# A graph layer on one core: edge windows fetched ahead of x, and the first 24 gathered rows prepared one pass earlier

## The chip, the cores and the metric

The kernel runs on one core of a Trainium2 chip. A core has five engines with instruction streams of their own: TensorE (PE, matrix products), VectorE (DVE), ScalarE (ACT), GpSimd (POOL) and SyncE (SP), which here only issues DMA transfers. They share an on-chip memory (SBUF) and the accumulators that PE writes (PSUM); transfers to and from DRAM run on 16 DMA engines. Semaphores order all of it. The metric is the device time of one execution in microseconds (us); lower is better.

## The reference

```python
h = jnp.maximum(_layernorm(x, axis=-1), 0.0)          # x: 6250 x 128
x_i, x_j = h[dst], h[src]                             # 206250 edges, sorted by dst
msg = jnp.concatenate([x_i, x_j - x_i], -1) @ W.T + b # W: 128 x 256
out = jax.ops.segment_max(msg, dst, num_segments=6250)
return x + jnp.where(jnp.isfinite(out), out, 0.0)
```

The product splits: a message is A[dst] + B[src] with A = h (W1 - W2)^T + b and B = h W2^T. A is the same for every edge of a node, so the kernel needs, for each node, the largest B row over its source nodes, and adds A and x at the end. Every node has an edge to itself.

## The kernel before, in words

Each of the 128 partitions (lanes) owns 49 neighbouring destination nodes (LD) and with them one window of 1792 neighbouring edges (WIN). For each edge a DVE or PE route takes the maximum:

- **Staging of edges** (lines 176 to 285, 477 to 498). The starts of the windows are counted from loads of dst (line 181, count on ACT at 271). Two indirect transfers of POOL fetch the source and destination numbers of every window (284 `swin`, 285 `dwin`). Keys follow (483 to 498): source divided by Q = 50 (quotient l and remainder q), destination relative to the lane. ACT writes the quotient in f32 (`big`, 483) with its bias `kbias`, DVE rounds it (490) and goes on in 16 bits.
- **Comparisons** (528 to 580). Edges of a lane that have the same destination and the same quotient collide. 41 shifted comparisons on DVE (`shift`, 535) are summed by PE into `dup` (524); between them stand, by a list written out by hand (`among`), the layer norm's statistics (`moments`, 292; `scales`, 298), and small steps of the normalisation and product (`micro`, taken by `ln`).
- **Normalisation and product** (416 to 475). For each pair of the 50 columns q: ACT normalises (`scaled`), PE transposes (`turn`), PE multiplies (`product`), ACT copies out; `remainder` writes the second half of a split of B. B goes to `Bt` in DRAM (448 to 460), A to `XA` in DRAM. Both pass through the four halves of `stage`. The bias comes as one more matmul (433), from `bsel` and `brow`. x is added to XA by an accumulating transfer of POOL (`add_x`, 444), group by group of ten columns, once SP has written the group; the last group's stands at line 702.
- **Compaction** (592 to 725). ACT takes the sign of `dup` (594), a scan counts (609), and 11 passes (`pass_`, 624) move the edges that collided to the front of each lane: bit i of the distance is done in pass i. Up to 420 of them (GR) are handled by gathering. Before pass 6 (EP), `early` (637) takes the first 48 (EW) aside: it joins 14 blocks (SETS) in a tree (651 to 654), writes the index `ridx` (655) and issues 48 gathers.
- **Gathered edges.** `gather_group` (144) issues up to 8 indirect transfers (line 87), each one row of B per lane, into a ring of 48 places (6 groups, GB) in `X`; `stream_step` (151) takes the running maximum on DVE (157) and sends it to `M` in DRAM (164). A place is used again when its steps are done. x itself lies in the same memory `X` before.
- **The other edges** are taken by products with one-hot matrices in the main loop: 325 pairs, each with one-hot columns (905, 906), four matmuls (983) and one DVE maximum (989). `more_rows` (922) weaves stream steps and gathers in: 10 steps before the loop (971), then up to a limit that grows with the pair (990). From row 206 on, gathers of finished rows of M into `R` (919) join POOL's queue.
- **The end** (1002 to 1024). The last rows are gathered, XA is read, results are transposed, combined and stored.
- **Checks** of the input's shape write `badc` (380, 384, 397, 737 to 764); if any fails, a slow path (1030) runs. It doesn't run here. `tick` (506) is a small PE load.

Every engine works its own list in the order written. SP's begins with dst, x's first ten columns (193), W, b, then copies that wait for `swin` and `dwin` (340), then the other x columns (342).

Of the kernel before, what the change touches and what calls it, by code (L numbers as in the profile page):

```python
# [8 lines left out]
F32 = mybir.dt.float32  # L9
# [10 lines left out]
P = 128  # L20
# [33 lines left out]
def gnn_kernel(tc, x, src, dst, W, b, out):  # L54
# [17 lines left out]
    EP = 6  # L72
    EW = GB * U
    SETS = (WIN - EW - (1 << EP)) // (2 << EP) + 1
    assert EW + (1 << EP) <= 2 << EP and SETS <= 16 and WIN % (2 << EP) == 0
# [17 lines left out]
    with ExitStack() as ctx:  # L93
# [13 lines left out]
        with ExitStack() as body:  # L107
# [58 lines left out]
            with ExitStack() as pre:  # L166
# [16 lines left out]
                bsrc = pool.tile([33, C], F32, name="bsrc")  # L183
# [60 lines left out]
                kbias = pool.tile([P, 1], F32, name="kbias")  # L244
                bsel = pool.tile([P, L], F32R, name="bsel")
                brow = pool.tile([P, 2 * C], F32R, name="brow")
                V.memset(kbias, (1 - Q) * 0.5 / Q)
                V.memset(bsel.bitcast(F32), 0.0)
                V.memset(brow.bitcast(F32), 0.0)
                for r in (0, 32):  # L250
                    V.memset(bsel[r:r + 1].bitcast(F32), 1.0)
# [33 lines left out]
                gather(dwin, dst.rearrange("(e o) -> e o", o=1), begin_i[:, 0:1])  # L285

# [27 lines left out]
                for r in (0, 32):  # L314
                    V.tensor_copy(brow[r:r + 1, C:], bsrc[r:r + 1])
                V.tensor_tensor(brow[32:33, C:], bsrc[32:33], brow[32:33, C:].bitcast(F32), ALU.subtract)
# [5 lines left out]
                moments(0, GQ)  # L322
                scales(0, GQ)()
                V.tensor_copy(identb, ident)
                neg = pool.tile([P, P], BF16, name="neg")
                V.tensor_scalar_mul(neg, identb, -100.0)
                negb = pool.tile([P, P], BF16, name="negb")
                V.tensor_scalar_mul(negb, identb, -1.0)
# [3 lines left out]
                V.tensor_copy(IQ, row[:, 0, :Q].rearrange("p (q o) -> p q o", o=1).to_broadcast([P, Q, NBLK]))  # L332
                V.tensor_copy(IL, row[:, 1, :LD].rearrange("p (q o) -> p q o", o=1).to_broadcast([P, LD, NBLK]))
                for i in range(NBLK):
                    V.tensor_scalar_add(IW[:, :, i], row[:, 1, :WN], float(near[i]))
                V.tensor_scalar(nbias, row[:, 0], -2.0, -1.0, op0=ALU.mult, op1=ALU.add)


                for j, w_ in enumerate((swin, dwin)):
                    S_.dma_start(SC[j:j + 1], w_[:1, :1])  # L340
# [102 lines left out]
                def add_x(q0):  # L443
                    G_.dma_start(out=XA_l[:, q0:q0 + GQ], in_=x_l[:, q0:q0 + GQ], accum_op=ALU.add)  # L444

                def remainder(k):
# [8 lines left out]
                    if o + 2 == GQ or q0 + GQ == Q and o + 2 == GQ - 4:  # L455
                        for to, j in ((Bt_l, g), (XA_l, 2 + g)):
                            for p0, p1 in PARTS:
                                S_.dma_start(to[p0:p1, q0 + o0:q0 + o + 2], stage[p0:p1, j, o0:o + 2])
                        if q0 + GQ < Q:
                            add_x(q0)  # L460
# [12 lines left out]
                scaled(0)  # L473
                ln(2)

# [7 lines left out]
                A_.activation(big, sq, AF.Identity, scale=1.0 / Q, bias=kbias)  # L483
                A_.activation(s16, sq, AF.Identity, bias=nthr)
                V.tensor_scalar(d16, dwin, nthr, None, op0=ALU.add)
                V.tensor_scalar(dlc, d16, 0.0, float(LD + 1), op0=ALU.max, op1=ALU.min)
                dlc64 = eq[0].bitcast(I16)
                lq = eq[1].bitcast(I16)
                V.tensor_scalar(dlc64, dlc, 64.0, None, op0=ALU.mult)
                V.tensor_scalar(vm, big, MAGIC, -(MAGIC + L), op0=ALU.add, op1=ALU.add)  # L490
                V.tensor_scalar(lq, vm, float(-Q), None, op0=ALU.mult)
                V.tensor_tensor(q2, s16, lq, ALU.add)
                V.tensor_tensor(KA[:, 64:], dlc64, q2, ALU.add)
                ln(2)
                A_.activation(big, sq, AF.Copy, scale=float(1 << PB))
                ln(2)
# [68 lines left out]
                among[4] += [sel_rows]  # L565
                later = {}
                for q0, at_ in ((GQ, (1, 2, 3, 5)), (2 * GQ, (8, 10, 11, 13)), (3 * GQ, (17, 19, 20, 22)),
# [5 lines left out]
                for i in range(1, 41):  # L573
                    among[i].append(lambda: ln(1))
# [16 lines left out]
                less = junk[0]  # L591
                for i in range(2):
# [3 lines left out]
                make_sel(30, 40)  # L596

# [39 lines left out]
                def early():  # L637
# [3 lines left out]
                    F, FM = (swin[:, j * 16 * EW:(j + 1) * 16 * EW].rearrange("p (m w) -> p m w", w=EW) for j in range(2))  # L641
# [15 lines left out]
                    for _ in range(GB):  # L657
# [23 lines left out]
                for i in range(5):  # L681
                    rest[i].append(lambda i=i: ln(4 if i < 4 else len(micro)))
# [13 lines left out]
                for i in range(11):  # L696
# [3 lines left out]
                    for f in rest[i]:  # L700
                        f()
                add_x(Q - GQ)
# [15 lines left out]
                                op1=ALU.bitwise_and)  # L718
                sdl = u[:, OV:GR + OV]
# [5 lines left out]
                V.tensor_scalar(s, s, -0.5, FMAX, op0=ALU.add, op1=ALU.mult)  # L725
                make_sel(40, Q)
# [4 lines left out]
                spread_begin()  # L731
                finite(w_sb, 2 * C, P, 18)
                finite(bsrc[:1], C, 1, 20)
                found()
                apart()
# [3 lines left out]
                V.tensor_scalar(badc[:, 4:5], over_, 0.0, None, op0=ALU.is_lt)  # L739
                V.tensor_tensor(less[:, 1:], d16[:, 1:], d16[:, :WIN - 1], ALU.is_lt)  # L740
# [11 lines left out]
                for v, op, o in ((VMAX, ALU.is_lt, badc[:L, 16:17]), (-VMAX, ALU.is_gt, badc[:L, 17:18])):  # L752
                    V.tensor_scalar(fin_[:L, :Q], mv[:, :, 1], v, None, op0=op, op1=ALU.add, accum_out=o)
                    V.tensor_scalar(o, o, -1.0, float(Q), op0=ALU.mult, op1=ALU.add)
                tick(8)

                sdl_f = pool.tile([P, 1], F32, name="sdl_f")
                heads = pool.tile([P, 2], F32, name="heads")
                V.tensor_copy(sdl_f, sdl[:, :1])
# [340 lines left out]
```

## Time and profile before

| | us |
|---|---|
| median of three runs | 774.2 |
| lowest and highest | 771.93 and 775.31 |
| the profiled execution | 775.43 |
| its span, first to last instruction | 773.6 |
| mean granted clock of TensorE | 0.943 |

The profile comes from one execution. A row of a timeline gives start, duration, engine, line, operation, what is written and read, and in brackets the idle time of the engine just before and what is inferred to have ended it. A row of groups gives count, busy time and mean duration in ns, then the idle time before. L87 is the line of a helper, so all gathers stand under it and are told apart by names.

### The profile page before, as it was taken

What the parts mean: (1) busy time and instruction counts of PE and PEld (TensorE: products, weight loads), DVE (VectorE), ACT (ScalarE), POOL (GpSimd) and SP (SyncE); (2) the same over time, 40 slices, a digit from 0 to 9 for tenths busy, and PEclk for the clock granted to TensorE, in tenths of its full rate; (3) what the DMA queues carried; (4) which work ended last, traced back from release to release, by engine and by line L of the source; (5) the groups of instructions that cost most, each with busy time, mean ns of one, the idle gap of its engine ahead of it and who ended that gap; (6) DMA issues with size and microseconds to landing.
All of it is one profiled execution on the core that took longest, in us unless ns stands there. A gap on an engine that the chain in (4) does not pass through costs nothing.

```text
span 773.6 us, 11963 instructions
## 1 busy us (share of the span) xinstructions
PE 642.1 (83%) x3643; PEld 466.6 (60%) x3643; DVE 720.9 (93%) x1304; ACT 482.9 (62%) x1035; POOL 504.0 (65%) x522
## 2 busy tenths in 40 slices
PE   0799884649999898899989898999989898996860
PEld 0455553537667676666767666766767576775750
DVE  6999799987999999999999999999999999997773
ACT  3655683226789999565666657575666667674500
POOL 4000003877777777777777777777777777777764
PEclk9999997759999999999999999999999999998875
DMA  6542444123443433334343243434343233433593
GB/s 196 133 101 67 101 104 108 46 61 94 109 116 103 117 104 92 104 106 116 106 117 101 83 114 104 116 106 115 104 116 101 83 113 103 116 106 106 160 227 123
DMA packets 83699, 85.05 MB, mean 110 GB/s; under 512 B 9996, under 2 KB 71554, under 8 KB 83372
## 3 DMA queue, kind: packets, MB, share of 16 engines
q1 hardware_dynamic: 66951, 47.36, 21.7%
q0 software_dynamic: 16080, 35.93, 17.5%
q10 hardware_dynamic: 596, 0.92, 0.4%
q8 instruction: 30, 0.49, 0.3%
q14 instruction: 42, 0.34, 0.1%
HBM read 46.76 MB, written 40.47 MB: 113 GB/s over the span
## 4 chain that ended last, share of the span: by engine, by line
DVE 25%; PE 16%; issue 15%; ACT 9%; DMA 9%; POOL 3%; DVEq 0%; POOLq 0%
DVE acc L989 15%; PE ps L983 9%; DVE X L157 6%; DMA X<-Bt,ridx 6%; ACT oh L906 5%; PE z L905 4%; ACT counted L996 4%; DMA R<-M,last_e 3%; PE pv L837 2%; POOL X L87 2%; POOL R L87 1%; DVE OHQ L800 1%; DVE acc L987 1%; DVE OHD L807 1%; DVE OHD L804 0%
## 5 line engine op out<-in xcount | busy, mean ns | idle before, releaser
L87 POOL DMA_INDIRECT X<-Bt,ridx x420 | 440.7, 1049 | 131.7 <-issue 45.4
L906 ACT ACTIVATE oh<-z 126x490 fp32r<-126x490 f32 (+1 forms) x650 | 340.1, 586 | 162.6 <-PE z L905 161.3
L983 PE MATMUL ps<-oh,Bp 126*128 126x490 f32 (+1 forms) x1300 | 392.5, 425 | 40.1 <-DVE acc L989 38.9
L989 DVE TENSOR_TENSOR acc<-acc,ps 128x980 f32<-128x980 f32 (+1 forms) x312 | 361.1, 1157 | 8.3 <-PE ps L983 6.8
L983 PEld LDWEIGHTS ps<-oh,Bp 126*128 126x128 f32 x1300 | 239.3, 193 | 135.0 <-DVE acc L989 90.8
L905 PE MATMUL z<-Vb,Sel 128*126 128x490 f16 (+1 forms) x650 | 195.3, 375 | 12.4 <-ACT oh L906 9.7
L157 DVE SCALAR_TENSOR_TENSOR X<-X,slim 128x128 f32<-128x128 f32 x419 | 146.8, 350 | 9.2 <-issue 7.6
L905 PEld LDWEIGHTS <-Sel 128*126 128x126 f16 x650 | 86.8, 142 | 32.1 <-issue 3.9
L837 PEld LDWEIGHTS <-OHQ 128*128 128x128 bf16 x910 | 62.5, 161 | 17.8 <-issue 16.9
L837 PE MATMUL pv<-OHD,OHQ 128*128 128x28 bf16 (+1 forms) x896 | 67.2, 228 | 4.5 <-DVE OHD L807 4.4
L444 POOL DMA_DIRECT2D XA<-in_x x5 | 4.5, 902 | 94.3 <-DMA XA<-acc 94.3
L800 DVE TENSOR_TENSOR OHQ<-T,IQ 128x1092 bf16<-128x1092 bf16 (+5 forms) x104 | 62.2, 605 | 0.0
L87 POOL DMA_INDIRECT R<-M,last_e x49 | 48.3, 985 | 17.0 <-issue 11.3
L996 ACT ACTIVATE counted<-lane_dl,nbias 128x556 bf16<-128x556 int32 x50 | 42.6, 851 | 0.1
L524 PE MATMUL dup<-T,identb 128*128 128x512 bf16 (+1 forms) x168 | 39.8, 363 | 3.0 <-DVE T L535 2.8
L436 PE MATMUL pm<-wT,hT 128*125 128x256 f32 x100 | 27.7, 402 | 2.7 <-ACT hT L425 2.6
L524 PEld LDWEIGHTS <-identb 128*128 128x128 bf16 x168 | 16.2, 99 | 18.8 <-issue 6.4
L633 DVE COPY_PREDICATED pk<-big,pk 128x1927 int32<-128x1927 int32 (+12 forms) x13 | 22.9, 1759 | 0.4
L436 PEld LDWEIGHTS pm<-wT,hT 128*125 128x125 f32 x100 | 19.5, 198 | 6.1 <-ACT hT L425 3.7
L419 ACT ACTIVATE hs<-X,nmr,rstd 125x128 f32<-125x128 f32 x50 | 22.0, 494 | 0.5 <-DVE nmr L306 0.5
L535 DVE TENSOR_TENSOR T<-KA,KB 128x1792 bf16<-128x1792 int16 x21 | 21.5, 1081 | 0.2 <-PE dup L524 0.2
L535 DVE TENSOR_TENSOR T<-KA 128x1792 bf16<-128x1792 int16 x20 | 20.8, 1080 | 0.0
(272 smaller groups left out, 452.1 us busy)
## 6 DMA issues: line engine op xcount, KB each, us to landing
M<-X SPq DMA_DIRECT2D x52, 512.0 KB
X<-Bt,ridx POOLq DMA_INDIRECT x420, 2.5
XA<-in_x POOLq DMA_DIRECT2D x5, 625.0 KB, 6.1
ownb<-Bt SPq DMA_DIRECT2D x12, 245.0 KB
X<-in_x SPq DMA_DIRECT2D x5, 560.0 KB
Bt<-acc SPq DMA_DIRECT2D x4, 560.0 KB
XA<-acc SPq DMA_DIRECT2D x4, 560.0 KB
out_x<-R SPq DMA_DIRECT2D x8, 224.0 KB
```

The lines of the kernel that those rows point to most:

```text
L87: G_.indirect_dma_start(out=o, out_offset=None, in_=table, in_offset=bass.IndirectOffsetOnAxis(ap=idx, axis=0))
L157: V.scalar_tensor_tensor(G[:, j], state["prev"], slim[:, k:k + 1], G[:, j], op0=ALU.min, op1=ALU.max)
L436: T_.matmul(pm[:L, j], hT[k % 2][:, j, :L], wT, start=False, stop=j == 1)
L524: T_.matmul(dup[:, c0:c1], w, e[:, c0:c1], start=first, stop=last)
L535: V.tensor_tensor(e, KA[:, 64:], i1, ALU.is_equal)
L800: V.tensor_tensor(OHQ[:, :nl, a:z], over(TQ, z - a), iq, ALU.is_equal)
L837: T_.matmul(o, w, m, start=False, stop=True, skip_group_check=True)
L905: T_.matmul(z[:L + 1, :n], Sel[:, i + j], Vb[t % 2][:, :n], start=True, stop=True)
L906: A_.activation(oh[:, :n], z[:L + 1, :n], AF.Relu)
L983: T_.matmul(ps[:, j, :n], Bp[:, e, i + j], oh[j][:, :n], start=e == 0, stop=e == 1)
L989: V.tensor_tensor(a, a, ps[:, :, :n], ALU.max)
L996: A_.activation(counted.bitcast(BF16)[:, :NS], lane_dl, AF.Sign, scale=2.0, bias=nbias[:, c:c + 1], accum_out=ends[:, c:c + 1])
```

## The change

In the order of the program:

- SP loads W and b first; x's first ten columns come after the copy that waits for `swin`.
- The constants `identb`, `neg`, `negb`, `IQ`, `IL`, `IW` and `nbias` are made on DVE right after the edge windows are requested; the first statistics move from there into the comparisons (at 0 and 1), as do the first steps of the normalisation. Two steps are taken at every fifth comparison.
- The quotient is made by DVE from the integers into 16 bits; ACT's `big` for packing moves to comparison 7.
- The bias matmul, `bsel`, `brow` and `kbias` go. SP fills XA with 6250 copies of b, POOL adds x in five accumulating transfers, and each group of A is added from `stage` by one more accumulating transfer.
- `early` runs before pass 5 with 24 rows (EP 5, EW 24, SETS 28); the other 24 rows of the ring are requested after the final index.
- Some checks move: those on W and on the variances beside ACT's sign pass, the head count ahead of the last part of `Sel`.
- 4 stream steps run before the loop instead of 10; in the loop at least min(3k + 7, 16) are done after pair k.

```diff
-    EP = 6
-    EW = GB * U
+    EP = 5
+    EW = 3 * U
...
-                load_x(0)
                 S_.dma_start(w_sb, W)
-                for r in (0, 32):
-                    S_.dma_start(bsrc[r:r + 1], at(b, 0, [[C, 1], [1, C]]))
+                S_.dma_start(bsrc, at(b, 0, [[C, 1], [1, C]]))
...
                 gather(swin[:, :WIN], src.rearrange("(e o) -> e o", o=1), begin_i[:, 0:1])
                 gather(dwin, dst.rearrange("(e o) -> e o", o=1), begin_i[:, 0:1])
+                V.tensor_copy(identb, ident)
...
+                V.tensor_scalar(nbias, row[:, 0], -2.0, -1.0, op0=ALU.mult, op1=ALU.add)
...
-                moments(0, GQ)
-                scales(0, GQ)()
...
                 for j, w_ in enumerate((swin, dwin)):
                     S_.dma_start(SC[j:j + 1], w_[:1, :1])
+                    if j == 0:
+                        load_x(0)
                 for q0 in range(GQ, Q, GQ):
                     load_x(q0)
+
+                S_.dma_start(XA, at(b, 0, [[0, N], [1, C]]))
...
-                    T_.matmul(pm[:L], bsel, brow.rearrange("k (o c) -> k o c", o=1).to_broadcast([P, 2, 2 * C]),
-                              start=True, stop=False)
                     for j in range(2):
-                        T_.matmul(pm[:L, j], hT[k % 2][:, j, :L], wT, start=False, stop=j == 1)
+                        T_.matmul(pm[:L, j], hT[k % 2][:, j, :L], wT, start=j == 0, stop=j == 1, skip_group_check=True)
...
-                def add_x(q0):
+                for q0 in range(0, Q, GQ):
                     G_.dma_start(out=XA_l[:, q0:q0 + GQ], in_=x_l[:, q0:q0 + GQ], accum_op=ALU.add)
...
+                        if o + 2 == GQ:
+                            G_.dma_start(out=XA_l[:, q0:q0 + GQ], in_=stage[:, 2 + g], accum_op=ALU.add)
...
-                A_.activation(big, sq, AF.Identity, scale=1.0 / Q, bias=kbias)
+                V.tensor_scalar(l16, sq, 1.0 / Q, (1 - Q) * 0.5 / Q, op0=ALU.mult, op1=ALU.add)
+                V.tensor_scalar(lq, l16, float(-Q), float(Q * L), op0=ALU.mult, op1=ALU.add)
+                V.tensor_scalar(vm, l16, float(-L), None, op0=ALU.add)
...
+                among[7] += [lambda: A_.activation(big, sq, AF.Copy, scale=float(1 << PB))]
...
+                spread_begin()
...
+                finite(w_sb, 2 * C, P, 18)
...
-                    for _ in range(GB):
+                    for _ in range(EW // U):
                         gather_group()
...
-                add_x(Q - GQ)
...
+                for _ in range(GB - EW // U):
+                    gather_group()
...
-                more_rows(10)
+                more_rows(4)
...
-                    more_rows(GR * (k + 1 - wait) // (len(pairs) - wait - early))
+                    more_rows(max(GR * (k + 1 - wait) // (len(pairs) - wait - early), min(3 * k + 7, 16)))
```

More of the change, by code (lines that the diff above doesn't have):

```diff
@@ L725, in gnn_kernel @@
                 V.tensor_scalar(s, s, -0.5, FMAX, op0=ALU.add, op1=ALU.mult)
+                sdl_f = pool.tile([P, 1], F32, name="sdl_f")
+                heads = pool.tile([P, 2], F32, name="heads")
+                V.tensor_copy(sdl_f, sdl[:, :1])
+                V.tensor_scalar(mask[:, NS:NS + GR], sdl, sdl_f, None, op0=ALU.is_equal, op1=ALU.add, accum_out=heads[:, :1])
+                V.scalar_tensor_tensor(heads[:, 1:], heads[:, :1], float(P), lane, op0=ALU.mult, op1=ALU.add)
+                p = ps_m.tile([P, 512], F32, name="pm")
+                T_.matmul(p[:P - 1, :1], ident[:, 1:], heads[:, 1:], start=True, stop=True)
+                V.tensor_scalar(badc[:, 5:6], heads[:, :1], float(MENDK), None, op0=ALU.is_gt)
+                V.memset(mend_i, 0)
                 make_sel(40, Q)
```

90 lines of the change are left out of this document (29 added, 61 removed).

## The prediction

> **What bounds the kernel now.** The page says that VectorE (DVE) is busy most; what GpSimd (POOL) does between its instructions decides.
>
> ```profile
> span 773.6 us, 11963 instructions
> PE 642.1 (83%) x3643; PEld 466.6 (60%) x3643; DVE 720.9 (93%) x1304; ACT 482.9 (62%) x1035; POOL 504.0 (65%) x522
> ```
>
> POOL looks free at 65%. Its groups in the stretch from 200 to 700 us (count, busy us and mean ns, idle before) say otherwise:
>
> ```profile
> L87 POOL DMA_INDIRECT X<-Bt,ridx x357 | 370.6, 1038 | 108.8 <-issue 35.0 <-DMA X<-Bt,ridx 26.2 <-DVE acc L989 25.9
> L87 POOL DMA_INDIRECT R<-M,last_e x15 | 14.9, 993 | 4.6 <-issue 3.0 <-DMA X<-Bt,ridx 1.5
> L87 POOL DMA_INDIRECT mend<-M,mend_i x1 | 0.9, 940 | 0.3 <-DMA X<-Bt,ridx 0.3
> ```
>
> Busy and idle add up to 500.1 of the 500 us, and 108.8 / 357 is 0.30 us of idle per gather: 373 gathers stand back to back, each with 0.30 us of issue. Whatever the releaser column names, POOL waits for nobody. The windows (us, then busy of PE, PEld, DVE, ACT, POOL) put DVE beside it:
>
> ```profile
> 175.00:200.00 25.00, 25.00 (x149) 19.02 (x147) 19.98 (x26) 15.59 (x30) 19.41 (x20) 0.95 0.30 84
> 350.00:400.00 50.00, 45.42 (x262) 33.20 (x261) 49.90 (x85) 31.65 (x61) 38.72 (x38) 1.00 0.41 113
> ```
>
> DVE is full too. Which of the two ends last? The timeline of DVE late in the loop:
>
> ```profile
> 710.02 0.35 DVE L157 SCALAR_TENSOR_TENSOR X<-X,slim 128x128 f32<-128x128 f32 x1 [4.02 <-issue]
> 722.89 0.40 DVE L157 SCALAR_TENSOR_TENSOR X<-X,slim 128x128 f32<-128x128 f32 x1 [3.55 <-issue]
> ```
>
> DVE stands 4.02 and 3.55 us before a stream step, waiting for its row. So the chain that ends the run is POOL's: 420 gathers of X in one row from the first, then the gathers of R, the output. The end moves by what POOL's queue gains; what DVE gains beyond that becomes more such waits.
>
> POOL's queue begins here (POOL's timeline, and DVE's up to the index that releases it):
>
> ```profile
> 128.79 0.99 POOL L87 DMA_INDIRECT X<-Bt,ridx  x1 [4.07 <-ACT KB L678]
> 130.08 1.72 POOL L87 DMA_INDIRECT X<-Bt,ridx  x1 [0.31 <-issue]
> 134.79 2.97 POOL L87 DMA_INDIRECT X<-Bt,ridx  x1 [0.30 <-issue]
> 140.82 0.98 POOL L87 DMA_INDIRECT X<-Bt,ridx  x1 [0.30 <-issue]
> ```
>
> ```profile
> 119.80 1.15 DVE L632 TENSOR_SCALAR big<-pk 128x1896 int32<-128x1896 int32 x1
> 120.98 2.26 DVE L633 COPY_PREDICATED pk<-big,pk 128x1896 int32<-128x1896 int32 x1
> ...
> 127.58 0.21 DVE L653 COPY_PREDICATED swin<-swin 128x48 int32<-128x48 int32 x1
> 127.83 0.19 DVE L655 TENSOR_SCALAR ridx<-swin 128x48 int32<-128x48 int32 x1
> ...
> 129.86 1.12 DVE L632 TENSOR_SCALAR big<-pk 128x1864 int32<-128x1864 int32 x1
> ```
>
> The first gather follows `ridx` (128.02) by 0.8 us. ACT, named as releaser, is not among its inputs.
>
> **The change, part by part.**
>
> *Start.* DVE and SP now:
>
> ```profile
> 13.97 0.29 DVE L309 TENSOR_TENSOR w<-w_sb 128x128 f32<-128x128 f32 x1 [3.28 <-DMA w_sb<-in_L_gnn_W]
> 15.39 2.03 DVE L294 BATCH_NORM_STATS2 stats<-X 125x6 f32<-125x128 f32 x10
> 17.34 0.75 DVE L296 BATCH_NORM_AGGREGATE mv<-stats 125x2 f32<-125x6 f32 x10
> 18.47 0.22 DVE L305 RECIPROCAL rstd<-rstd 125x10 f32<-125x10 f32 x1 [0.37 <-ACT rstd L300]
> 18.80 0.22 DVE L324 CAST identb<-ident 128x128 bf16<-128x128 f32 x1
> 21.63 1.15 DVE L485 TENSOR_SCALAR d<-pk,nthr 128x1792 int16<-128x1792 int32 x1
> 22.82 0.63 DVE L486 TENSOR_SCALAR dlc__175<-d 128x1792 bf16<-128x1792 int16 x1
> 25.26 1.09 DVE L490 TENSOR_SCALAR vm<-big 128x1792 bf16<-128x1792 f32 x1 [1.15 <-ACT big L483]
> 29.91 2.09 DVE L535 TENSOR_TENSOR T<-KA 128x1792 bf16<-128x1792 int16 x2
> ```
>
> ```profile
> 16.80 0.25 SPq L340 DMA_DIRECT2D SC<-swin  x1
> 19.97 0.21 SPq L340 DMA_DIRECT2D SC<-pk  x1
> ```
>
> The SP copies wait for the two edge windows, so `swin` is there at 16.8 and `dwin` at 20.0. The constants (18.80 to 21.63, 2.83 us) go into the 3.28 us of idle ahead of 13.97 and are hidden. The keys now take 29.91 - 21.63 = 8.28 us; without the wait of 1.15 and the f32 `vm` of 1.09, with an int32 pass of 1.15 and an int16 one of 0.63, they take 7.8. They can start when `swin` lands. Two opposite effects bear on that: 0.64 MB of x no longer goes first, and the constants now run on DVE while POOL writes the descriptors of both gathers. I leave it at 16.8 (bounds 15.5 and 18.3). `dwin` is wanted 3.7 us after `swin`, later than 20.0. The first comparison then starts at 24.6, 5.3 earlier. The statistics of the first ten x columns (2.03 + 0.75 + 0.22 + about 0.2) move behind it, so 3.1 comes back: **2.2 us gained**, bounds 0.7 and 3.5. x itself now stands on SP behind the copy that waits for `swin`, and behind it wait the copy of `dwin`, the other x chunks, XA's fill and the Bt stores; it is issued at 17 and wanted near 26, and if it came later, DVE would stand. The dropped bias rows counted before 15.39; DVE now waits for `swin` at that place, so they bring nothing.
>
> *Comparisons.* DVE waits for TensorE (PE) twice, then for ACT's sign pass:
>
> ```profile
> 85.00 3.10 DVE L535 TENSOR_TENSOR T<-KA,KB 128x1792 bf16<-128x1792 int16 x3 [0.23 <-PE dup L524]
> 88.72 1.09 DVE L542 TENSOR_TENSOR T<-dlc__175 128x1792 bf16<-128x1792 bf16 x1 [0.62 <-PE dup L524]
> 93.52 0.35 DVE L598 TENSOR_SCALAR flow<-level,listed 128x128 f32<-128x128 f32 x1 [2.32 <-ACT T L594]
> ```
>
> PE loses one bias matmul per product, so the 0.85 us goes and PE's lag behind DVE shrinks a little: **1.0 us** (bounds 0 and 1.4). The checks moved into the 2.32 us wait take no time there and free about 1.7 us behind the passes, for DVE alone.
>
> *Early rows.* `ridx` for 24 rows is written without pass 5 in front (1.15 + 2.26 = 3.4 us) but with one level more in the tree (28 sets instead of 14: two instructions like the 0.21, 0.4 us). So POOL starts 2.2 + 1.0 + 3.4 - 0.4 = 6.2 us earlier. Beside passes 6 to 8 the second to fifth gathers took 130.08 to 140.82, 2.7 us each instead of 1.25. Pass 5 now lies beside gathers too: in its 3.4 us 1.3 get through instead of 2.7, **1.8 us lost** (bounds 0 and 3.4). The second half of the ring is issued after line 717's index, well before POOL has done 24. Bt's last store, already ahead of the first gather, moves with the normalisation chain and no longer shares its queue with XA's.
>
> *XA.* One accumulation stood among the gathers:
>
> ```profile
> 198.88 1.02 POOL L444 DMA_DIRECT2D XA<-in_x  x1
> 200.20 1.04 POOL L87 DMA_INDIRECT X<-Bt,ridx  x1 [0.30 <-DVE X L157]
> ```
>
> It goes: **1.0 us**. The ten accumulations of the new kernel are issued ahead of the first gather, in POOL's idle time; what waits behind them on POOL is the gathers, and the fill of XA that they wait for is a rival below.
>
> *Behind the passes (DVE only).* The head count's wait on PE goes, and fewer rows are run before the loop:
>
> ```profile
> 160.03 0.16 DVE L766 CAST mend_i<-pm 127x1 int32<-127x1 f32 x1 [1.18 <-PE pm L763]
> 171.99 3.44 DVE L157 SCALAR_TENSOR_TENSOR X<-X,slim 128x128 f32<-128x128 f32 x9
> ```
>
> DVE reaches the loop 2.2 + 1.0 + 1.7 + 1.2 - 0.4 = 5.7 us earlier, and six rows of 0.35 us move into the stretch where PE is full and DVE has 5 us idle (175 to 200): 7.8 in all. That is more than POOL gains, so POOL still ends last.
>
> **Sum:** 2.2 + 1.0 + 3.4 - 0.4 - 1.8 + 1.0 = 5.4 us. The profiled execution took 775.4 (its span 773.6 and 1.8 outside it) and would take 770.0; against the median of 774.2, **768.8**.
>
> **The rivals.**
>
> *The shared port costs more.* A gather beside pass 7 took 2.97 us, against 0.98 alone. If such passes stop POOL wholly, pass 5 costs 3.4 instead of 1.8, and the 2.83 us of constants delay both edge gathers by as much: 5.4 - 1.6 - 2.8 = 1.0 gained, 773.2. Against it: four gathers did finish beside three passes, and the constants are mostly small. The Trainium skill (SBUF — State Buffer, Who interferes with whom) states that a DVE instruction in a two-port mode or with two SBUF inputs and a GpSimd one hold the port exclusively, the second fully blocked. By that rule the sum is this rival's; the stretched gathers agree with a lock per instruction, not with a block through the whole stretch.
>
> *XA's chain holds the normalisation (slower).* XA is first filled with 6250 rows of bias; the five additions of x wait for that, and the first addition of a stage buffer for x's. ACT writes that buffer again for the eleventh pair of columns. Queue rows (packets, MB, share) of 20 to 32 us, which holds the last four of x's five loads, of 213 to 217 us (stores of 512 B rows) and of 52 to 59 us (one addition), and ACT's copy of that pair:
>
> ```profile
> q1 hardware_dynamic: 636, 2.55, 84.5%
> ```
>
> ```profile
> q1 hardware_dynamic: 1544, 0.78, 72.6%
> ```
>
> ```profile
> q0 software_dynamic: 144, 0.64, 53.7%
> ```
>
> ```profile
> 74.25 0.37 ACT L451 COPY acc<-pm 125x256 f32<-125x256 f32 x1 [0.59 <-PE pm L449]
> ```
>
> Packets of 512 B go at 1544 / (4 x 0.726) = 532 per us, so the fill takes 11.7 us behind x's load (near 31) and ends at 43; each addition takes 0.537 x 7 = 3.8 us, six with 2 us of latency 25: landed at 68, before 74. ACT waits from 74, PE two products (6 us) later, DVE three comparisons after that, at 83. So it decides once the fill ends after 58, at 2.3 times my rate; at three times it ends at 66, the addition lands at 91, and DVE loses 8: 777. The copies between two places in DRAM are not in this trace, hence its chance. The Trainium skill (DMA: Bandwidth & Descriptors, Why a DMA increments its semaphore by 16 and not by 1) lets a DMA use the largest number of engines up to 16 that divides its outer size, 10 for 6250; an estimate by it is 18.7 us, ending at 50, short of the point.
>
> *More.* Pass 5 costs gathers nothing and `swin` lands at 15.5: 5.4 + 1.8 + 1.3 = 8.5, 765.7.
>
> *It does not do what it says.* The keys start no earlier because the edges land as much later as they are wanted sooner; 5.4 - 2.2 = 3.2, 771.0.
>
> **How the numbers follow.** Forecast 0.55, port 0.15, XA's chain 0.13, more 0.10, no earlier keys 0.07. The measurement tells about 0.5%, 3.9 us, from no change. The forecast's terms leave it on the faster side four times in five (0.44); with "more" and a little of the others 0.56 faster. Slower is XA's chain and a remainder, 0.15; within 0.5%, 0.29. The range goes from 764.5, below "more", to 776, which leaves out most of XA's chain.
>
> **What would show it.** First comparison near 24.6; first gather of X near 122.6; the gathers from there to the last in one unbroken row, its last one near 718; DVE's waits before stream steps late in the loop longer than 4.02 and 3.55. ACT standing before L451 near 74 and DVE before L535 near 83 would show XA's chain. A first gather at 122 with an end that has not moved would prove wrong that POOL's queue sets the end.

## The result, and the profile after

The changed kernel takes 839.6 us (median of 4 runs, 838.13 to 840.56) against 773.9 (4 runs, 771.93 to 775.31): the ratio is 1.0849, with a 95% interval of 1.0819 to 1.0879. It is 66 us slower. The forecast was 768.8, its range 764.5 to 776.0, and the rival nearest to what happened gave 777.

The page of the profiled execution (839.02 us) begins so. The rows of slices cover 837.2 / 40 = 20.9 us with each figure.

```profile
span 837.2 us, 11852 instructions
PE 639.8 (76%) x3618; PEld 463.6 (55%) x3618; DVE 721.1 (86%) x1299; ACT 481.6 (58%) x1034; POOL 511.5 (61%) x527
...
DVE  7996011899988999999999999999999999999683
ACT  3463002683146799995757576666666666667320
POOL 4000020017777777777777777777777777777764
...
GB/s 181 148 37 37 36 144 150 61 100 50 65 88 80 108 101 91 120 100 95 98 116 104 126 103 110 102 110 101 110 98 114 98 114 98 110 102 122 120 236 132
```

DVE is as busy as before in microseconds (721.1 against 720.9), so it got no more work; standing was added. From the third to the fifth slice, about 42 to 105 us, the transfers move 37 GB/s, and from the fifth to the seventh, 84 to 147 us, DVE and ACT all but stand still. From there on the run looks as before: POOL's groups from 250 to 750 us in the changed kernel again fill the stretch, 0.30 us of idle per gather.

```profile
L87 POOL DMA_INDIRECT X<-Bt,ridx x358 | 369.8, 1033 | 109.1 <-issue 37.5 <-DMA X<-Bt,ridx 23.5 <-DVE acc L973 23.5
L87 POOL DMA_INDIRECT R<-M,last_e x15 | 16.5, 1098 | 4.6 <-DMA X<-Bt,ridx 2.4 <-issue 2.1
```

What stood? SP's timeline of the changed kernel (start, duration of the issue, line, transfer), where L331 is the fill of XA, L362 a small store of zeros and L444 the stores of B:

```profile
24.59 0.85 SPq L331 DMA_DIRECT2D XA<-in_L_gnn_b  x1
25.55 79.90 SPq L362 DMA_DIRECT2D Bt<-zero  x1
105.54 80.25 SPq L444 DMA_DIRECT2D Bt<-acc  x12
```

The fill itself is issued in 0.85 us. The next issue, a store of 11 KB, takes 79.90 us: SP gets it out at 105.45, when most of the fill is done. All stores of B are written behind it. POOL's, ACT's and DVE's timelines show who waits for the fill and for those stores (L431 adds x, L446 adds A, L428 and L438 copy into the four halves of `stage`, L305 is a step of the statistics, L516 a comparison, L523 the last one):

```profile
116.92 4.48 POOL L431 DMA_DIRECT2D XA<-in_x  x5 [100.92 <-DMA XA<-in_L_gnn_b]
...
190.81 0.99 POOL L87 DMA_INDIRECT X<-Bt,ridx  x1 [2.37 <-DVE ridx L643]
```

```profile
118.32 0.37 ACT L428 COPY acc<-pm 125x256 f32<-125x256 f32 x1 [45.93 <-DMA Bt<-acc]
139.37 0.37 ACT L438 COPY acc<-pm 125x256 f32<-125x256 f32 x1 [20.20 <-DMA XA<-acc]
```

```profile
16.13 1.09 DVE L470 TENSOR_SCALAR T<-swin 128x1792 int16<-128x1792 int32 x1 [2.31 <-DMA swin<-in_src,begin_i]
...
23.66 1.08 DVE L516 TENSOR_TENSOR T<-KA 128x1792 bf16<-128x1792 int16 x1
...
118.93 0.22 DVE L305 RECIPROCAL rstd<-rstd 125x10 f32<-125x10 f32 x1 [43.47 <-ACT rstd L300]
142.83 1.09 DVE L516 TENSOR_TENSOR T<-KA,KB 128x1792 bf16<-128x1792 int16 x1 [18.77 <-PE dup L505]
...
153.00 1.09 DVE L523 TENSOR_TENSOR T<-dlc__172 128x1792 bf16<-128x1792 bf16 x1 [0.39 <-PE dup L505]
```

The fill ends near 117 instead of 43. ACT stands twice: 45.93 us for a store of B, which is behind the fill on SP's queue, then 20.20 us for the addition to XA, which is behind the fill on POOL's. DVE stands 43.47 us for ACT, then 18.77 us for PE, which waits for ACT's copies. The last comparison starts at 153.00 instead of 88.72, 64.3 later, the first gather at 190.81 instead of 128.79, 62.0 later, and the last one at 786.84 instead of 722.97, 63.9 later. The whole loss lies before the gathers; behind them nothing is given back.

The rate of the fill: DMA queues of the changed kernel from 40 to 100 us (packets, MB, share of the 16 engines).

```profile
q1 hardware_dynamic: 4243, 2.17, 33.8%
```

4243 packets in 60 us are 71 rows of 512 B per us, where the forecast had 532 from stores out of SBUF. And the packets fill only a third of the time of 16 engines.

For some runs below the kernel before itself took 1064 to 1089 us on the same chip; their times are marked as not compared, and of their traces only what lies before the loop is used.

### The profile page after: what moved, and what is told of

Its sections match the earlier page's. It is cut to its first block, busy times and chain, and to the rows that moved or that the text cites. A ratio compares the mean times of both kernels' runs of the same rounds, so it can differ in the third digit from the quotient of the medians.

```text
span 837.2 us, 11852 instructions
## 1 busy us (share of the span) xinstructions
PE 639.8 (76%) x3618; PEld 463.6 (55%) x3618; DVE 721.1 (86%) x1299; ACT 481.6 (58%) x1034; POOL 511.5 (61%) x527
## 5 line engine op out<-in xcount | busy, mean ns | idle before, releaser
L967 PE MATMUL ps<-oh,Bp 126*128 126x490 f32 (+1 forms) x1300 | 393.0, 425 | 40.5 <-DVE acc L973 39.5
L889 PE MATMUL z<-Vb,Sel 128*126 128x490 f16 (+1 forms) x650 | 196.0, 376 | 12.9 <-ACT oh L890 10.3
L157 DVE SCALAR_TENSOR_TENSOR X<-X,slim 128x128 f32<-128x128 f32 x419 | 145.0, 346 | 7.6 <-issue 5.5
L431 POOL DMA_DIRECT2D XA<-in_x x5 | 4.5, 1579 | 100.9 <-DMA XA<-in_L_gnn_b 100.9
L505 PE MATMUL dup<-T,identb 128*128 128x512 bf16 (+1 forms) x168 | 42.8, 385 | 14.8 <-DVE T L516 14.8
L436 PE MATMUL pm<-Bp,negI 125*125 125x256 f32 x25 | 10.4, 414 | 48.6 <-ACT acc L428 48.6
L516 DVE TENSOR_TENSOR T<-KA,KB 128x1792 bf16<-128x1792 int16 x21 | 22.0, 1083 | 23.6 <-PE dup L505 23.6
L446 POOL DMA_DIRECT2D XA<-acc x5 | 4.8, 967 | 60.8 <-ACT Bp L439 56.3
L305 DVE RECIPROCAL rstd<-rstd 125x10 f32<-125x10 f32 x5 | 1.1, 210 | 43.6 <-ACT rstd L300 43.5
L428 ACT COPY acc<-pm 125x256 f32<-125x256 f32 x25 | 9.6, 383 | 45.9 <-DMA Bt<-acc 45.9
L436 PEld LDWEIGHTS pm<-Bp,negI 125*125 125x125 f32 x25 | 5.2, 208 | 52.4 <-ACT acc L428 51.4
L505 PEld LDWEIGHTS <-identb 128*128 128x128 bf16 x168 | 16.8, 105 | 31.5 <-issue 19.3
```

The costliest lines, as they stand in the source:

```text
L157: V.scalar_tensor_tensor(G[:, j], state["prev"], slim[:, k:k + 1], G[:, j], op0=ALU.min, op1=ALU.max)
L436: T_.matmul(pm[:L, :, :C], negI[:L, :L], Bp[:L, 0, 2 * k:2 * k + 2], start=False, stop=True, skip_group_check=True)
L505: T_.matmul(dup[:, c0:c1], w, e[:, c0:c1], start=first, stop=last)
L516: V.tensor_tensor(e, KA[:, 64:], i1, ALU.is_equal)
L889: T_.matmul(z[:L + 1, :n], Sel[:, i + j], Vb[t % 2][:, :n], start=True, stop=True)
L967: T_.matmul(ps[:, j, :n], Bp[:, e, i + j], oh[j][:, :n], start=e == 0, stop=e == 1)
```

## The experiments

**Which part costs the time.** Two kernels split the change: the kernel before with the XA part alone (`before_xa`), and the change without it (`xa_as_before`, run twice).

```diff
 # before_xa, on the kernel before
+                S_.dma_start(XA, at(b, 0, [[0, N], [1, C]]))
...
-                    T_.matmul(pm[:L], bsel, brow..., start=True, stop=False)
...
-                        for to, j in ((Bt_l, g), (XA_l, 2 + g)):
+                        if o + 2 == GQ:
+                            G_.dma_start(out=XA_l[:, q0:q0 + GQ], in_=stage[:, 2 + g], accum_op=ALU.add)
```

> The kernel before with only the change's XA part: no bias matmuls, XA filled from the one row of b in DRAM behind x's loads, ten POOL additions. Theory 1: it loses what the changed kernel lost, the fill ends near 118, ACT waits for Bt near 72, and the time is 835 to 850. If the loss needs another part of the change as well, it stays under 820.

> The changed kernel with its whole XA part undone: bias by matmul again, XA written by SP and x added by POOL group by group, as in the kernel before; all other parts of the change stay. Theory 1 (the fill of XA alone costs, through the queue behind it): no wait of DVE over 2 us among the comparisons, first gather of X near 122, 767 to 771 us. Theory 2 (another part of the change has a share of the 65 us): above 776 us.

> The changed kernel with its XA part undone, again, for its time. With the fill gone and one POOL addition back among the gathers (1.0 us) and the bias matmuls back (1.0 us), theory 1 gives 2 us more than the variant filled from SBUF: 768 to 773. If XA's ten additions cost something of their own in the other variant, this one is the faster of the two.

`before_xa` took 842.85 us in its one run, beside 773.96 (median of 23 runs) for the kernel before on the same chip: 68.9 more. Its two long ACT waits are those of the changed kernel (us in total, times, longest):

```profile
ACT acc L440 <- DMA Bt<-acc: 47.7, 1, 47.7
ACT acc L450 <- DMA XA<-acc: 21.1, 1, 21.1
```

`xa_as_before` took 1075.12 us against 1067.22 (not compared). `xa_as_before2` took 775.37 us (12 runs, 770.9 to 777.66), ratio 1.001, interval 0.9995 to 1.0025. So the XA part makes the whole loss, and the rest of the change brings nothing by itself, where my terms gave 5.4 - 1.0 (XA) - 0.85 (bias) = 3.5 us. Why nothing, this kernel's timelines show (POOL's first gathers, then two comparisons of DVE):

```profile
121.58 1.18 POOL L87 DMA_INDIRECT mend<-M,mend_i  x1 [3.89 <-DVE mend_i L642]
128.34 1.30 POOL L87 DMA_INDIRECT X<-Bt,ridx  x1 [5.58 <-DMA Bt<-acc]
```

```profile
24.87 1.08 DVE L528 TENSOR_TENSOR T<-KA 128x1792 bf16<-128x1792 int16 x1
...
89.12 1.09 DVE L535 TENSOR_TENSOR T<-dlc__173 128x1792 bf16<-128x1792 bf16 x1 [0.62 <-PE dup L517]
...
126.29 0.18 DVE L655 TENSOR_SCALAR ridx<-swin 128x24 int32<-128x24 int32 x1
```

The first comparison is 5.0 us earlier than before, the last one 0.4 later. The statistics that moved in between take 3.1 us of that, and with the bias matmuls still there and the steps of the product packed closer, DVE also waits 1.9 us for PE (0.85 before) and 1.1 us for ACT. And where the index is ready at 126.47, the gather waits until 128.34 for the last store of B. A new wait has taken the place of pass 5.

**The source of the fill.** The same 6250 rows of 512 B, but out of a copy of b in 125 partitions of SBUF, on the same queue at the same place (`fill_sbuf`, run twice).

```diff
+                S_.dma_start(bb, at(b, 0, [[0, L], [1, C]]))
...
-                S_.dma_start(XA, at(b, 0, [[0, N], [1, C]]))
+                for p0, p1 in PARTS:
+                    S_.dma_start(XA_l[p0:p1], bb[p0:p1].rearrange("l (o c) -> l o c", o=1).to_broadcast([p1 - p0, Q, C]))
...
-                S_.dma_start(bb, at(b, 0, [[0, L], [1, C]]))
```

> The changed kernel, but XA is filled with the same 6250 rows of 512 B from a copy of b in 125 partitions of SBUF, in two transfers, instead of from the one row in DRAM. Theory 1, with the source row in DRAM as what is slow: the fill ends near 45 us (532 rows per us as the stores of M), no wait of ACT for a Bt store, 766 to 771 us. Rival 1a (6250 rows are too many for one queue, whatever their source): the fill still takes over 60 us and the time stays above 815. Rival 1b (the ten accumulating transfers hold the stage buffers): the fill is short, but ACT waits over 5 us before its copies to stage, above 776.

> The changed kernel with XA filled from a copy of b in 125 partitions of SBUF, as before, on another chip for its time. The fill ended near 45 us in the first look, so ACT shouldn't wait for a Bt store nor DVE among the comparisons. If the fill was all that the change lost and my steps of the forecast hold, 766 to 771 us, with the first gather of X near 122. If the rest of the change brings nothing, within 3 us of the kernel before; if it loses too, above 777.

`fill_sbuf` took 1057.83 us against 1067.22 (not compared); POOL's additions start at 45.87. `fill_sbuf2` took 772.49 us (12 runs, 770.37 to 775.15), ratio 0.9978, interval 0.9966 to 0.9989. DMA queue from 34 to 40 us, and POOL, in its trace:

```profile
q1 hardware_dynamic: 3994, 2.04, 112.5%
```

```profile
45.39 4.48 POOL L433 DMA_DIRECT2D XA<-in_x  x5 [28.70 <-DMA XA<-bb]
```

3994 / 6 = 666 rows per us, a little over the forecast's 532. Beside the source only the load of that copy differs, which moves from late in the kernel to its start, and the 67 us are gone. So the fill's source is the cause, and the version with it is the only one here that beats the kernel before, by 0.2%.

**Engines or queue.** `fill_16` keeps the row in DRAM, and splits the fill so that 16 engines share it; `fill_act` only issues it from ACT's queue.

```diff
 # fill_16
-                S_.dma_start(XA, at(b, 0, [[0, N], [1, C]]))
+                K = N // 16
+                S_.dma_start(XA[:16 * K].rearrange("(a k) c -> a k c", k=K), at(b, 0, [[0, 16], [0, K], [1, C]]))
+                S_.dma_start(XA[16 * K:], at(b, 0, [[0, N - 16 * K], [1, C]]))
 # fill_act
-                S_.dma_start(XA, at(b, 0, [[0, N], [1, C]]))
+                A_.dma_start(XA, at(b, 0, [[0, N], [1, C]]))
```

> The changed kernel with the same fill from the one row in DRAM cut as 16 x 390 rows and a rest of 10, so that its outer size is divisible by 16. If the number of engines sets the pace (10 for 6250 by the Trainium skill's page on DMA), the fill takes 86 x 10 / 16 = 54 us and ends near 86; the time is then about 30 us shorter than 839.6. If the one source row sets it, the fill takes 86 us as now and the time stays within 5 us of 839.6.

> The changed kernel with the fill issued by ACT instead of SP; nothing else moves. It takes as long as now (ends near 117), but Bt's stores no longer stand behind it. If SP's blocked queue is what costs, the wait of 45.9 us for Bt disappears and the time falls below 790. If POOL's additions, which wait for the fill too, bind just as late, ACT waits for XA's addition instead, until about 139, and the time stays above 825.

Queues of `fill_16` from 40 to 100 us, and its POOL:

```profile
q1 hardware_dynamic: 4083, 2.09, 56.2%
```

```profile
120.65 4.48 POOL L433 DMA_DIRECT2D XA<-in_x  x5 [104.24 <-DMA XA<-in_L_gnn_b]
```

68 rows per us, and the additions at 120.65: the number of engines does not set this fill's pace. (1142.08 us in its one run, not compared.) The packets take 0.562 x 16 x 60 / 4083 = 132 ns each where they took 76 in the changed kernel: more engines at work, longer packets, the same rate. The Trainium skill (DMA: Bandwidth & Descriptors, Why a DMA increments its semaphore by 16 and not by 1) was weighed in the prediction for 10 engines; whether 10 or 16 take part makes no difference to this fill, so its rule doesn't explain the slowness.

In `fill_act` (1148.86 us in its one run, not compared) ACT waits for no store of B, but DVE waits for x's loads, though they are on another queue. SP's timeline, DVE's, and the queues from 30 to 90 us (q10 is ACT's):

```profile
23.50 89.02 SPq L191 DMA_DIRECT2D X<-in_x  x8
```

```profile
58.05 1.06 DVE L294 BATCH_NORM_STATS2 stats<-X 125x6 f32<-125x128 f32 x5 [32.41 <-DMA X<-in_x]
111.83 1.06 DVE L294 BATCH_NORM_STATS2 stats<-X 125x6 f32<-125x128 f32 x5 [47.77 <-DMA X<-in_x]
```

```profile
q10 hardware_dynamic: 4153, 2.13, 12.4%
q1 hardware_dynamic: 148, 0.59, 2.7%
```

4153 rows of the fill and 148 packets of SP's queue share 60 us. The slow transfer on one queue holds up the other, as long as it lasts. The Trainium skill (DMA: Bandwidth & Descriptors, Queues, rings and completion order) says that SP's and ACT's queues are rings on the same 16 engines, which take turns between them; the trace agrees as far as it goes, with 28 rows of the fill to one packet of SP's queue; whether the taking of turns or SP's slow issues hold x's loads, no run here shows. So `fill_act` doesn't part the two waits; the table below does.

**One row, or DRAM to DRAM?** `fill_rows` copies 6250 different rows of x into XA, from DRAM to DRAM, so it has the fill's count and size of rows but another source. It leaves the bias out of the result.

```diff
-                S_.dma_start(XA, at(b, 0, [[0, N], [1, C]]))
+                for r in range(2):
+                    S_.dma_start(at(XA, r * C, [[2 * C, N // 2], [1, C]]), at(x, r * C, [[2 * C, N // 2], [1, C]]))
```

> The changed kernel with 6250 rows of 512 B copied into XA from 6250 different rows of x in DRAM (even rows, then odd ones) in place of the one row of b; x is still added, so XA holds twice x and no bias. If reading one and the same row is what is slow (14 ns per row on ten or sixteen engines alike), the copy runs at several hundred rows per us, ends near 45, and the time is that of the variant filled from SBUF. If any copy from DRAM to DRAM in 512 B rows is slow, it ends near 117 and the time stays near 840.

It took 786.88 us in its one run, 12.9 above the kernel before. Its queue from 34 to 58 us, then POOL, ACT and DVE:

```profile
q1 hardware_dynamic: 5087, 2.60, 35.8%
```

```profile
63.60 4.48 POOL L432 DMA_DIRECT2D XA<-in_x  x5 [47.30 <-DMA XA<-in_x]
```

```profile
88.58 0.37 ACT L439 COPY acc<-pm 125x256 f32<-125x256 f32 x1 [13.37 <-DMA XA<-acc]
```

```profile
92.05 1.09 DVE L517 TENSOR_TENSOR T<-KA,KB 128x1792 bf16<-128x1792 int16 x1 [12.42 <-PE dup L506]
...
101.55 1.09 DVE L524 TENSOR_TENSOR T<-dlc__172 128x1792 bf16<-128x1792 bf16 x1 [0.39 <-PE dup L506]
```

5087 / 24 = 212 rows per us: three times the rate of the one row, a third of that from SBUF. The shares tell where the difference to SBUF lies. A packet takes 0.358 x 16 x 24 us / 5087 = 27 ns here, and 1.125 x 16 x 6 us / 3994 = 27 ns from SBUF, so a copy from DRAM to DRAM costs no more per row; but the share is 35.8% against 112.5% (above 100% because packets overlap), about five engines' work instead of 16. (Each of the two transfers has 3125 rows, and five is the largest number up to 16 that divides it; no run here varies that.) So it is the one row that costs: with it the rate stays at 68 to 71, whether the packets take 76 ns (the change), 132 ns (`fill_16`) or 29 ns (`fill_act`).

Here the first wait, that for B's stores, is absent, and the second alone makes the loss, in just the way of the rival: the fill is over at 63.60, the additions take until 88.58 (25.0 us, forecast 25), ACT and then DVE stand.

**How late may the fill be?** `fill_mix` takes 1250 of the rows from b in DRAM and 5000 from SBUF, out of the same early copy.

```diff
-                S_.dma_start(XA, at(b, 0, [[0, N], [1, C]]))
+                for p0, p1 in PARTS:
+                    S_.dma_start(XA_l[p0:p1, GQ:], bb[p0:p1]...to_broadcast([p1 - p0, Q - GQ, C]))
+                S_.dma_start(XA_l[:, :GQ], at(b, 0, [[0, L], [0, GQ], [1, C]]))
```

> The fill of XA as a dose. Ten of the fifty columns (1250 rows of 512 B) are filled from the one row of b in DRAM, the other forty (5000 rows) from a copy of b in SBUF. At 72 rows per us for the first kind and 680 for the second, the fill takes 17.4 + 7.4 = 24.7 us behind x's loads (about 33) and ends near 57; POOL's five additions of x start near 58, between 45.4 (all from SBUF) and 63.6 (rows of x). The prediction's rule, that the fill decides once it ends after 58: no wait of DVE, time as with all rows from SBUF, about 772.5. What the run with rows of x shows (fill's end 63.6, copy into the stage buffer released 25 us later, DVE standing 12.4): the point lies at about 63.6 - 12.4 = 51, DVE stands about 7 us before a comparison between 79 and 90, and the time is 772.5 + 7 = 779.5.

It took 1095.31 us against 1088.93 (not compared); the timeline of DVE up to the last comparison serves:

```profile
88.54 1.09 DVE L519 TENSOR_TENSOR T<-KA,KB 128x1792 bf16<-128x1792 int16 x1 [8.68 <-PE dup L508]
...
98.07 1.09 DVE L526 TENSOR_TENSOR T<-dlc__173 128x1792 bf16<-128x1792 bf16 x1 [0.39 <-PE dup L508]
```

| kernel | additions of x start | last comparison | later than with SBUF | point from which it costs |
|---|---|---|---|---|
| `fill_sbuf2` | 45.39 | 87.05 | 0 | |
| `fill_mix` | 60.64 | 98.07 | 11.0 | 49.6 |
| `fill_rows` | 63.60 | 101.55 | 14.5 | 49.1 |
| the change | 116.92 | 153.00 | 66.0 | 51.0 |

The last column is the second less the fourth. Each microsecond beyond about 50 costs one, all the way to 117, so the waits for B's stores lie inside those for XA's additions and add nothing of their own. The additions started at 60.64 instead of 58, so by the prediction's point of 58 they could have cost 2.6 us at most; 11.0 decide for 50.

**The rest of the sum.** Three kernels on the base of `fill_sbuf`, each run three times (none compared).

```diff
 # sbuf_ep6
-    EP = 5
-    EW = 3 * U
+    EP = 6
+    EW = GB * U
...
 # sbuf_tail, in the loop over comparisons, and beside the first passes
-                    among[i].append(lambda i=i: ln(2 if i % 5 == 4 else 1))
+                    among[i].append(lambda i=i: ln((2 if i % 5 == 4 else 1) if i < SH - 2 else 0))
...
-                    rest[i].append(lambda i=i: ln(4 if i < EP - 1 else len(micro)))
+                    rest[i].append(lambda i=i: ln(5 if i < 3 else 4 if i < EP - 1 else len(micro)))
 # sbuf_rows10
-                more_rows(4)
+                more_rows(10)
...
-                    more_rows(max(GR * (k + 1 - wait) // (len(pairs) - wait - early), min(3 * k + 7, 16)))
+                    more_rows(GR * (k + 1 - wait) // (len(pairs) - wait - early))
```

> The kernel with the fill from SBUF, but with the early rows as before: 48 rows ahead of pass 6, all 48 gathers issued there. The prediction's price of this step was 3.4 - 0.4 - 1.8 = 1.2 us, so the time is 1.2 longer than 772.5: 773.7. The trace of the kernel with the fill from SBUF says that its first eight gathers took 16.1 us instead of 13.4 beside passes 5 to 8, so the step brings 3.0 - 2.7 = 0.3 us: 772.8, with the first gather of X near 127.5 and the 24th near 166.5. If POOL stands still through a whole pass, the step brings nothing or less: 772.0 to 772.5.

> The kernel with the fill from SBUF, without steps of the normalisation and product at the last two comparisons; three more stand beside the first three passes instead. If the 0.9 us between the last comparison and ACT's sign pass is lost because TensorE runs a product's four matmuls ahead of the last sums of dup, the sum of the two halves comes 0.9 us earlier, the passes too, the first gather of X near 123.5 instead of 124.4, and the time is 772.5 - 0.9 = 771.6. If Bt's last store, which ends the chain of steps, is what holds the first gather, it stays at 124.4 or later and the time at 772.5 or above.

> The kernel with the fill from SBUF, but with 10 stream steps before the loop and the pace in the loop as before. The prediction: POOL ends last, so the six rows that DVE runs later bring nothing and taking that back costs nothing, 772.5, with DVE's waits before late stream steps shorter. The rival, DVE ends last: six rows of 0.35 us, 2.1 us longer, 774.6.

The second runs had sharper expectations, the third ones the same again:

> The kernel with the fill from SBUF and the early rows as before (48 rows ahead of pass 6). The prediction's price of the step, 3.4 - 0.4 - 1.8 = 1.2 us: 772.5 + 1.2 = 773.7. The places of the 24th gather, counted from the last comparison (77.0 us with this early part, 76.5 with that of the change): 0.5 us, 773.0.

> The kernel with the fill from SBUF, without steps at the last two comparisons. Its index is ready 1.2 us earlier, counted from the last comparison, but the first gather of X stands behind the last addition to XA and the gather of mend on POOL's queue and is issued 0.2 us earlier only. By POOL's queue: 772.5 - 0.2 = 772.3. By DVE's progress: 772.5 - 1.2 = 771.3.

> The kernel with the fill from SBUF, with 10 stream steps before the loop and the pace as before. POOL ends last (the prediction): no change, 772.5, POOL's busy and idle time between 200 and 700 us add up to 500 again, and DVE's waits before late stream steps are shorter than 5.6 us in total. DVE ends last: 2.1 us longer, 774.6.

> The kernel with the fill from SBUF and the early rows as before. By the prediction's price of that step 1.2 us more than 772.5: 773.7; by the places of the 24th gather 0.5 us more: 773.0.

> The kernel with the fill from SBUF, without steps at the last two comparisons. By POOL's queue, in which the last addition to XA stands ahead of the gathers, 0.2 us less: 772.3; by DVE's progress 1.2 us less: 771.3.

> The kernel with the fill from SBUF, 10 stream steps before the loop and the pace as before. POOL ends last: no change, 772.5. DVE ends last: six rows of 0.35 us, 2.1 us more, 774.6.

The medians were 1080.24, 1075.45 and 1063.9 us (`sbuf_ep6`), 1076.07, 1068.57 and 1057.86 (`sbuf_tail`) and 1061.3, 1081.84 and 1060.33 (`sbuf_rows10`), beside 1088.93, 1089.37 and 1063.81 for the kernel before. Places counted from the start of the last comparison, mean of the runs and their extremes (the row of the change's early part is that of `fill_sbuf` and the three `sbuf_rows10`, which are alike up to there):

| early part | first gather | 24th gather |
|---|---|---|
| of the change | 37.4 (37.3 to 37.6) | 76.3 (75.9 to 76.7) |
| as before (`sbuf_ep6`) | 40.5 (40.5 to 40.5) | 76.8 (76.6 to 77.0) |
| without steps at the end (`sbuf_tail`) | 37.0 (36.9 to 37.2) | 75.5 (75.3 to 75.8) |

The early rows start 3.1 us sooner, and at the 24th gather 0.5 is left, with ranges that overlap. In `fill_sbuf2` the two places are 37.3 and 77.8 us, in the kernel before 40.1 and 78.0. `sbuf_tail` gets its index 1.2 us sooner on the mean, and the first gather only 0.4; POOL's and DVE's rows of its first run show what holds it:

```profile
122.14 0.84 POOL L448 DMA_DIRECT2D XA<-acc  x1 [10.99 <-ACT Bp L441]
123.28 1.06 POOL L87 DMA_INDIRECT mend<-M,mend_i  x1 [0.30 <-DMA Bt<-acc]
124.65 1.75 POOL L87 DMA_INDIRECT X<-Bt,ridx  x1 [0.30 <-issue]
```

```profile
91.91 0.34 DVE L588 TENSOR_SCALAR flow<-level,listed 128x128 f32<-128x128 f32 x1 [0.30 <-ACT T L580]
...
123.12 0.18 DVE L645 TENSOR_SCALAR ridx<-swin 128x24 int32<-128x24 int32 x1
```

The index is there at 123.30, but on POOL's queue stands the last addition to XA, which waits for ACT's last step, and behind it the gather of `mend`, then the first of X. Whether POOL or DVE ends the loop, `sbuf_rows10` was to tell, and its times don't; in its three traces POOL's gathers of X stand idle 399 to 422 us in all, against 128 in `fill_sbuf2`, so they don't show the loop in question either. That stays open.

## Why the prediction was wrong, point by point

- **The step that failed** is the size in the rival "XA's chain holds the normalisation": "Packets of 512 B go at 1544 / (4 x 0.726) = 532 per us, so the fill takes 11.7 us ... and ends at 43". It goes at 71 per us and ends at 117. The rate came from stores out of SBUF; the text said that copies between two places in DRAM were not in the trace, and gave no upper bound from that, only a chance of 0.13, so the forecast's sum has nothing for it. What made it slow was not the copy between two places in DRAM, which takes 27 ns per packet like one out of SBUF (`fill_rows`), but that every row is read from the same place. With 117 in its own working, additions of 25 us and a point of 58, the rival gives some 59 us, near the 66 measured. The mechanism was right, a term of it 7.5 times too fast.
- **The rival's point** "once the fill ends after 58" is 50. It counted 9 us from ACT's standing to DVE's. In `fill_rows` ACT stands from 75.2 and DVE from 79.6, so 4.4, and when ACT goes on at 88.58, DVE does at 92.05, 3.5 later: what cover there is, the way back takes again.
- **The order of the waits**: the signs named ACT's standing near 74, for the addition to XA. The first wait was another, for B's stores behind the fill on SP's queue. The prediction listed those stores as standing behind the fill and priced nothing for it. By the table above it cost nothing beyond XA's chain, which ends later.
- **XA's gain of 1.0 us**: right in size once the fill is quick. From the 25th to the 49th gather `fill_sbuf2` took 31.1 us against 32.2. But "in POOL's idle time" was wrong for the last of the ten: it stands ahead of the first gather (`sbuf_tail`).
- **Start, 2.2 us**: `swin` landed at 16.13 in the changed kernel (forecast 16.8) and at 16.78 in `fill_sbuf2`. There `dwin` was late by 0.91 us, which the forecast had excluded, so the first comparison came at 25.15 instead of 24.6; with 3.1 us of statistics given back the last one came at 87.05, 1.7 us earlier than before.
- **Comparisons, 1.0 us**: nothing. The two waits on PE are 0.91 us together (0.85 before), and 0.9 more is lost behind the last one, from its start to `flow` 5.68 us instead of 4.80. `sbuf_tail` brings that stretch to 4.44: a product's matmuls stood ahead of the last sums. Rows of `fill_sbuf2`:

```profile
83.56 3.10 DVE L518 TENSOR_TENSOR T<-KA,KB 128x1792 bf16<-128x1792 int16 x3 [0.52 <-PE dup L507]
87.05 1.09 DVE L525 TENSOR_TENSOR T<-dlc__173 128x1792 bf16<-128x1792 bf16 x1 [0.39 <-PE dup L507]
...
92.73 0.35 DVE L588 TENSOR_SCALAR flow<-level,listed 128x128 f32<-128x128 f32 x1 [1.55 <-ACT T L580]
```

- **Early rows, 3.4 - 0.4 = 3.0 us**: right; the index was ready at 124.12 instead of 128.02, and these 3.9 us are 3.0 and the 0.8 left of the two steps above. **1.8 lost beside pass 5**: about 2.7. POOL's timeline of `fill_sbuf2`:

```profile
124.39 0.99 POOL L87 DMA_INDIRECT X<-Bt,ridx  x1 [0.33 <-DVE ridx L645]
125.68 1.53 POOL L87 DMA_INDIRECT X<-Bt,ridx  x1 [0.30 <-issue]
127.52 3.15 POOL L87 DMA_INDIRECT X<-Bt,ridx  x1 [0.31 <-issue]
130.98 3.10 POOL L87 DMA_INDIRECT X<-Bt,ridx  x1 [0.30 <-issue]
134.38 2.96 POOL L87 DMA_INDIRECT X<-Bt,ridx  x1 [0.30 <-issue]
137.65 2.42 POOL L87 DMA_INDIRECT X<-Bt,ridx  x1 [0.30 <-issue]
```

  Each gather of 3.15 and 3.10 with its 0.30 is as long as a pass (3.4): one gets through per pass, not 1.3. The first eight are busy for 16.1 us instead of 13.4. The second to the fifth, 1.53 to 3.15 us long, each end 0.11 or 0.12 us after the TENSOR_SCALAR (L622) that opens a pass on DVE (at 127.10, 130.56, 133.96 and 137.23). The Trainium skill's exclusive lock (SBUF — State Buffer, Who interferes with whom) would have cost 3.4; the trace lies between that and my 1.8, near the middle.
- **The sum**: 5.4 us were forecast, and of them 3.0 stand at the 49th gather of `fill_sbuf2` (197.20 instead of 200.20), 1.35 at the last (721.62 instead of 722.97), and 1.5 in the medians (772.49 against 773.96). In its profiled execution the 151st to the 200th gather are busy for 52.8 us, against 51.3 before and 51.1 in the changed kernel with the same loop; that part varies between runs, and its cause is open.
- **What bounds the kernel**: POOL's unbroken row is there in the changed kernel and in `fill_sbuf2` as before, and a delay of 62.0 us of its first gather moved its last by 63.9 and the median by 66. That the end moves with this row's start is shown for a delay. For a gain it is not: the profiled execution of `fill_sbuf2` has its first gather 4.4 us earlier and its last 1.35, but its span is 773.5 against 773.6. That DVE has room beside POOL is not shown either: its late waits before stream steps were forecast to grow, and came to 7.1 us in all in `fill_sbuf2` against 8.2 before.

## What to carry to other kernels

A transfer whose kind the trace does not contain has no rate: bound it from the slowest row there is, or time it alone, and work a rival's price out for the whole range, since here the point at which it begins to cost (50 us) was close to what the quick rate gave (43 to 45). A constant that is to be spread over a large array in DRAM goes out of SBUF, and what is issued behind a long transfer on the same queue is counted as late as that transfer. A step taken off the path helps only up to the next thing in line: here the last store of B, then the last addition on POOL's queue.

## What the runs showed of the hardware

- Rows of 512 B into DRAM go at 666 per us from SBUF and at 212 from different rows in DRAM. A packet takes 27 ns in both; in the second about a third as many engines are at work.
- When all are read from one row in DRAM, they go at 68 to 71 per us, whether their packets fill 12.4%, 33.8% or 56.2% of the time of 16 engines. So the engines are not what is full. What is, no run here shows.
- An issue on SP's queue behind such a transfer took 79.90 us, though the slow transfer's own issue took 0.85. With the slow transfer on another queue DVE stood 32.41 and 47.77 us for x's loads.
- Indirect gathers of POOL went through at one per pass beside DVE's passes (a TENSOR_SCALAR and a predicated copy over 1800 to 1900 columns), 3.15 us instead of 0.94 to 0.99.
